# A gated cross-attention layer with a routed feed-forward part on one Trainium2 core: where the first batches' feed-forward part is done, the last row sums, and the opening loads

## The chip, the cores and the metric

The kernel runs on one core of a Trainium2 chip, as one program from its first load to its last store. The metric is device time in microseconds (us). A core has five engines with a queue of instructions each: TensorE (PE; its weight loads are listed apart as PEld), VectorE (DVE), ScalarE (ACT), GpSimd (POOL) and SyncE (SP). SP, ACT and POOL also issue DMA transfers. Each queue runs in its own order, and an instruction that waits holds up all that stand behind it. Products are accumulated in eight PSUM banks of 128 x 512 numbers.

## What is computed

Four batches of 256 tokens (x, 512 wide) attend to 1601 context rows each. 32 query heads share 8 key and value heads, four to one. Then each token goes through a base product and two of eight small experts. All of it is in float32.

```python
def _L0_xattn_ref(query, kv, Wq, bq, Wkv, bkv, Wo, bo):
    scale = 1 / sqrt(128)
    q = (query @ Wq + bq).reshape(B, L, 8, 4, 128)
    k_, v_ = jnp.split(kv @ Wkv + bkv, 2, axis=-1)
    k, v = k_.reshape(B, Lk, 8, 128), v_.reshape(B, Lk, 8, 128)
    scores = jnp.einsum('blkgd,bmkd->bkglm', q, k) * scale
    attn = jax.nn.softmax(scores, axis=-1)
    o = jnp.einsum('bkglm,bmkd->blkgd', attn, v).reshape(B, L, 4096)
    return o @ Wo + bo

def _L0_ffn_ref(x, base_W, router_W, lora_A, lora_B):
    base = jnp.einsum('bsd,od->bso', x, base_W)
    probs = jax.nn.softmax(jnp.einsum('bsd,ed->bse', x, router_W), axis=-1)
    top_vals, top_idx = jax.lax.top_k(probs, 2)
    rw = top_vals / jnp.sum(top_vals, axis=-1, keepdims=True)
    w_dense = jnp.sum(jax.nn.one_hot(top_idx, 8) * rw[..., None], axis=-2)
    mid = jnp.einsum('bsd,edr->bser', x, lora_A) * w_dense[..., None]
    return base + 2.0 * jnp.einsum('bser,erd->bsd', mid, lora_B)

x = x + jnp.tanh(g_xattn[0]) * _L0_xattn_ref(_layernorm(x), ctx_4096, Wq, bq, Wkv, bkv, Wo, bo)
x = x + jnp.tanh(g_ffn[0]) * _L0_ffn_ref(_layernorm(x), base_W, router_W, lora_A, lora_B)
```

## The kernel before

A *group* is one key head h of one batch b and one half l of its tokens: the four query heads of 128 tokens each make 512 columns (W). There are 4 x 8 x 2 = 64 groups, and the loop over `heads` and l runs them in order. A group's scores are 13 products (12 context tiles of 128 rows and one of 65), one PSUM bank each (`score_unit`, L880). ACT copies them to SBUF (L887) into tiles named p, two context tiles to one p, seven p to a group. DVE takes the maximum over the p (tile mx, `fold`, L806 to L812), spreads it to all partitions (`spread`, L845 to L839, result mb), and subtracts it (L915). ACT takes the exponential in place (L918), and TensorE multiplies with the values (`av_unit`, L967) while the next group's scores are made. DVE adds the same p up (tile sm, again `fold` and `spread`, with small copies on POOL) and scales the result by the inverse sums (`normalize`, L1017). ACT adds the value bias (oT, L1020), TensorE projects with the output weights (po, L1033), and DVE adds that to x in the tile xa (L1040). There are nine buffers for p, so that a copy of the next group's scores may have to wait until DVE has added up a p of the group before.

Between two groups lies a *window* of other work, held as tasks: projection, queries of the next head (pq, L531), keys and values of the next pair of heads (pxk, pxv and others), the next batch's context and x, and the feed-forward part. The order on TensorE, DVE and ACT is written out by hand (`manual_schedule`): a planner in the kernel keeps a clock per engine with costs of its own, gives each task a share of the windows before it is due, and takes the step that is ready first. `flush` does the same at the end without windows. DMA issues on SP and POOL are placed by the compiler's scheduler.

**Feed-forward part** (`ffn_steps`), for each of the eight tiles of 128 tokens: row statistics and normalisation on DVE (fn, L265 to L272), four transposes (pt_f, L248), a product with LoRA A and the router weights (pm, L1093), routing on DVE (`weigh`, L1114 to L1130) and one exponential on ACT (L1106), one transpose (pmt, L1140), the base product (py, L1085) and the LoRA B product into the same bank (L1152), the sum into xa (L1153) and the store. The first three batches' parts run in the windows of the batch that follows; the last batch's runs at the end. Its weights (base_t, ra, lb) stay in SBUF from the start: `ffn_weight_steps` loads them in the opening and transposes the base weights in the first groups.

**The last group** (7,1 of batch 3) has its p in the place of the context (p_last). It has no sums on DVE: after each value product, a product of the same p with a matrix of ones adds the sums up on TensorE (su, L980), 13 of them. `turn_over` turns these sums round (L1002 to L1005). The group before it (7,0) still uses DVE and POOL. The output weights wo have one buffer; `load_wo` of a head is called after the projection of the head before.

**The opening** loads 13 context tiles of batch 0 one at a time on SP (`load_first`, L1314), the first key weights and the bias on ACT's queue (L300, L220), and the first value weights, x, query and output weights on SP. TensorE transposes each tile (pt_ctx). The first key product (pk, L575) needs the short tile 12 and tiles 0 to 2.

Of the kernel before, what the change touches and what calls it, by code (L numbers as in the profile page):

```python
# [27 lines left out]
def flamingo_kernel(  # L28
# [190 lines left out]
    def load_small():  # L219
        nc.scalar.dma_start(bias[0:NHEAD], bq.rearrange("(h p) -> h p", p=P))  # L220
        nc.scalar.dma_start(bias[NHEAD:NBIAS], bkv.rearrange("(h p) -> h p", p=P))
        nc.gpsimd.dma_start(gates[:, 0:1], g_xattn.partition_broadcast(P))
        nc.gpsimd.dma_start(gates[:, 1:2], g_ffn.partition_broadcast(P))
        nc.gpsimd.dma_start(bo_b, bo.partition_broadcast(P))
# [95 lines left out]
    def load_wo(b, h):  # L320
        o = pool.tile([P, G, D], F32, tag="wo", name=f"wo_{b}_{h}", bufs=1)
# [6 lines left out]
    base_t = const.tile([P, NC, D], F32, name="base_t")  # L328
    ra = const.tile([P, NC, E * R + E], F32, name="ra")
    lb = const.tile([E * R, D], F32, name="lb")  # L330

    router_s = pool.tile([P, NL, D], F32, tag="xa", name="router_s")

    def ffn_weight_steps():
        staged = {}

        def load(o):
            n = P if o < NC else E

            if o == NC:  # L340
                s = router_s[:, 0, :]
            else:
                s = pool.tile([P, D], F32, tag="stage", name=f"base_{o}", bufs=STAGE)
# [3 lines left out]
        def begin():  # L347
            for c in range(NC):
                nc.gpsimd.dma_start(
                    ra[:, c, : E * R].rearrange("p (e r) -> p e r", r=R),  # L350
                    lora_a[:, c * P : (c + 1) * P, :].rearrange("e p r -> p e r"),
                )
            nc.sync.dma_start(lb, lora_b.rearrange("e r d -> (e r) d"))
            load(0)

        def step(o):
            def run():
                if o < NC:
                    load(o + 1)
                    dst, n = base_t[:, :, o * P : (o + 1) * P], P  # L360
                else:
                    dst, n = ra[:, :, E * R :], E
                transpose_rows(staged.pop(o), n, dst, f"base_{o}")
            return NC * TR_COST, LAG_DMA, run, True

        return [(0, 0, begin)] + [step(o) for o in range(NC + 1)]
# [7 lines left out]
    def x_steps(b):  # L374


        def begin():
            xa = pool.tile([P, NL, D], F32, tag="xa", name=f"xa_{b}")
# [516 lines left out]
    last = (B - 1, NKV - 1, NL - 1)  # L895
    assert (NPAIR - 1) * 2 * W <= NC * 2 * HW

    def softmax(key):
# [10 lines left out]
        for j, tiles in enumerate(pairs):  # L909
# [12 lines left out]
            if key != last:  # L922
                first = NPAIR - FULL // 2
                ns = 0 if j <= first else 1230 if j > first + 1 else 1970 if first else 1230
                later("sum", "v", ns, ("exp", key, j), lambda j=j: sum_piece(key, j), ("sum", key, j))
        if key != last:
            later("sum", "v", 0, 0.0, lambda: sum_spread(key), ("sums", key))

    def sum_piece(key, j):
        if j == 0:  # L930
            nm = "_".join(map(str, key))
            acc_t[key] = pool.tile([P, 2, W], F32, tag="sm", name=f"sm_{nm}", bufs=1)
# [18 lines left out]
    def av_unit(key, j):  # L951
# [22 lines left out]
        if key == last:  # L974

            if j == 0:
                sum_t[key] = bank(f"su_{nm}")
            for k, i in enumerate(pairs[j]):
                r = rows[i]
                nc.tensor.matmul(  # L980
                    sum_t[key],
                    ones[:r],
                    p_t[key][j][:r, k, :],
                    start=(j == 0 and k == 0),
                    stop=(j == NPAIR - 1 and k == len(pairs[j]) - 1),
                )
        if j == NPAIR - 1 and key != last:
            done["av", key] = clock["now"] + SEM
        elif key == last and j == NPAIR - 1:
            turn_over(key)  # L990

    def av_step(key, j):

        return 2 * len(pairs[j]) * mm_cost(W), ("exp", key, j), lambda: av_unit(key, j), j == 0

    def turn_over(key):

        nm = "_".join(map(str, key))
        rb = pool.tile([P, W], F32, tag="stage", name=f"rb_{nm}", bufs=STAGE)
        tr = pool.tile([P, W], F32, tag="stage", name=f"tr_{nm}", bufs=STAGE)  # L1000
        m = small.tile([P, NB], F32, tag="quadm", name=f"quadm_{nm}", bufs=2)
# [458 lines left out]
```

## Time and profile before

| what | value |
|---|---|
| median of three runs | 2665.49 us (2664.94 to 2667.97) |
| the profiled execution | 2665.57 us, of which its span 2663.8 us |
| mean granted TensorE clock | 0.997 |
| DVE's additions and maxima over p (sm, mx) | each about 1.22 us for 128 x 1024 numbers |
| ACT's copies of scores (L887) | 820, 0.59 us each, 463.4 us |
| TensorE's score products | 1664 passes, two to a product |
| mean DMA rate | 39 GB/s over the span |

The span runs from the first to the last instruction on the core. The other 1.8 us of the profiled execution lie around it. A float32 product is listed as two passes over TensorE, so that "x8" in a row is four products; rows overlap by the time a product takes to drain, so the time a step costs is read from one row's start to the next one's. The page shows the span in 40 slices, the busy share in tenths, and the granted clock; a full slice is 66.6 us:

```profile
PE   8999999999999999999999999999999999999997
DVE  2787877888878778778878878788887787888785
ACT  2544444454444344445444444444544444444441
PEclk9999999999999999999999999999999999999998
```

TensorE is nearly full everywhere but in the first and the last slice; DVE is at 70 to 80%.

### The profile page before, as it was taken

Reading aid. Unit: us, or ns where it says so; the run is one execution under the profiler, and the core shown is the slowest. Engines: PE = TensorE matmul, PEld = TensorE weight load, DVE = VectorE, ACT = ScalarE, POOL = GpSimd, SP = SyncE. Lnnn points to the kernel's source line nnn. Section 1 sums busy time; section 2 is a strip of 40 time slices with the busy share of each in tenths; the row PEclk is TensorE's granted clock in tenths of the full one; section 3 lists DMA queues with packets and bytes.
Section 4 is the critical chain, followed back from the end, with each engine's and each line's share of the span. In section 5 each row is a group of like instructions: output and inputs, shape, how many; then the busy total and the mean of one; then the engine's idle time right before and its main releaser. Section 6 shows DMA issues by size and latency. Waiting matters only on the chain.

```text
span 2663.8 us, 25411 instructions
## 1 busy us (share of the span) xinstructions
PE 2614.0 (98%) x9127; PEld 1480.4 (56%) x9127; DVE 2101.9 (79%) x3074; ACT 1200.5 (45%) x1920; POOL 92.3 (3%) x404
## 2 busy tenths in 40 slices
PE   8999999999999999999999999999999999999997
PEld 6555565655655556556555555556565564655543
DVE  2787877888878778778878878788887787888785
ACT  2544444454444344445444444444544444444441
POOL 0000000000000000000000000000000000000000
PEclk9999999999999999999999999999999999999998
DMA  3101111120111011112001010111210010100000
GB/s 127 53 17 40 40 32 40 40 74 24 40 32 40 25 39 40 40 32 89 24 24 40 32 56 8 40 40 44 70 40 21 28 48 32 40 25 24 32 16 24
DMA packets 78263, 104.72 MB, mean 39 GB/s; under 512 B 3324, under 2 KB 36140, under 8 KB 78136
## 3 DMA queue, kind: packets, MB, share of 16 engines
q1 hardware_dynamic: 76728, 102.01, 12.1%
q8 instruction: 72, 1.18, 0.2%
q0 software_dynamic: 272, 0.53, 0.1%
q10 hardware_dynamic: 1136, 0.55, 0.1%
q14 instruction: 55, 0.45, 0.1%
HBM read 100.98 MB, written 2.10 MB: 39 GB/s over the span
## 4 chain that ended last, share of the span: by engine, by line
PE 77%; DVE 15%; ACT 5%; issue 1%; POOL 1%; DMA 1%; SPq 0%; ACTq 0%; POOLq 0%; DVEq 0%
PE av L967 20%; PE sc L880 20%; PE po L1033 8%; PE pq L531 6%; PE pxk L665 5%; PE pxv L676 4%; DVE p L915 4%; PE pk L575 3%; ACT p L887 3%; PE pyk L665 2%; PE pyv L676 2%; DVE sm L812 2%; DVE mx L812 2%; ACT p L918 1%; PE pzk L665 1%
## 5 line engine op out<-in xcount | busy, mean ns | idle before, releaser
L880 PE MATMUL sc<-qT,kT 128*128 128x512 f32 (+1 forms) x1664 | 776.1, 592 | 7.7 <-ACT p L887 4.8
L887 ACT COPY p<-sc 65x512 f32<-65x512 f32 x820 | 463.4, 590 | 679.6 <-PE sc L880 348.4
L967 PE MATMUL av<-p,v 65*128 65x512 f32 x1640 | 766.1, 592 | 3.0 <-ACT p L918 3.0
L967 PEld LDWEIGHTS av<-p,v 65*128 65x128 f32 x1640 | 309.3, 190 | 382.6 <-issue 377.5
L880 PEld LDWEIGHTS sc<-qT,kT 128*128 128x128 f32 (+1 forms) x1664 | 306.3, 186 | 379.6 <-issue 334.4
L812 DVE TENSOR_TENSOR mx<-mx,p 128x1024 f32<-128x1024 f32 x252 | 308.8, 1226 | 237.8 <-ACT p L887 235.6
L918 ACT ACTIVATE p<-p 65x512 f32<-65x512 f32 x442 | 434.6, 995 | 124.6 <-DVE p L915 116.4
L915 DVE TENSOR_TENSOR p<-p,mb 65x512 f32<-65x512 f32 x442 | 481.8, 1137 | 0.2
L812 DVE TENSOR_TENSOR sm<-sm,p 128x1024 f32<-128x1024 f32 x252 | 307.2, 1219 | 1.3
L1033 PE MATMUL po<-wo,oT 128*128 128x512 f32 x512 | 231.7, 596 | 5.3 <-DMA wo<-in_L_xattn_Wo_dram 5.3
L531 PE MATMUL pq<-xnT,wq 128*128 128x256 f32 x1024 | 231.5, 379 | 0.0
L531 PEld LDWEIGHTS pq<-xnT,wq 128*128 128x128 f32 x1024 | 193.0, 190 | 38.6 <-issue 6.5
L1033 PEld LDWEIGHTS po<-wo,oT 128*128 128x128 f32 x512 | 95.5, 191 | 109.8 <-issue 105.8
L703 ACT ACTIVATE kT<-pxk,biasT 128x384 f32<-128x384 f32 (+1 forms) x120 | 60.7, 526 | 174.9 <-PE pxk L665 174.9
L706 ACT COPY v<-pxv 128x384 f32<-128x384 f32 x120 | 57.0, 475 | 166.7 <-PE pxv L676 166.7
L829 POOL COPY quad_sm<-quad_sm 32x16 f32<-32x16 f32 x189 | 46.6, 246 | 2363.9 <-DVE quad_sm L825 2217.4
L538 ACT ACTIVATE qT<-pq,biasT 128x256 f32<-128x256 f32 x128 | 60.6, 474 | 149.9 <-PE pq L531 149.3
L806 DVE TENSOR_TENSOR mx<-p,p 128x1024 f32<-128x1024 f32 x63 | 77.2, 1226 | 57.2 <-ACT p L887 57.2
L676 PE MATMUL pxv<-wv,T 128*128 128x128 f32 x720 | 91.4, 277 | 9.4 <-ACT v L706 9.4
L676 PEld LDWEIGHTS pxv<-wv,ctxT 128*128 128x128 f32 x720 | 88.7, 192 | 20.2 <-issue 18.4
L575 PE MATMUL pk<-ctxT,wk 128*128 128x417 f32 (+1 forms) x256 | 90.9, 509 | 2.8 <-ACT ctxT L250 1.5
L676 PEld LDWEIGHTS pxv<-wv,T 128*128 128x128 f32 x720 | 86.3, 192 | 12.4 <-ACT v L706 11.7
(158 smaller groups left out, 2284.4 us busy)
## 6 DMA issues: line engine op xcount, KB each, us to landing
wq<-in_L_xattn_Wq_dram SPq DMA_DIRECT2D x32, 1024.0 KB, 5.3
wo<-in_L_xattn_Wo_dram SPq DMA_DIRECT2D x32, 1024.0 KB, 5.3
ctx<-in_ctx_dram SPq DMA_DIRECT2D x48, 256.0 KB, 2.7
wk<-in_L_xattn_Wkv_dram SPq DMA_DIRECT2D x30, 256.0 KB, 2.9
wv<-in_L_xattn_Wkv_dram SPq DMA_DIRECT2D x30, 256.0 KB, 3.0
xa<-in_x_dram SPq DMA_DIRECT2D x4, 512.0 KB, 3.7
out_dram<-xa SPq DMA_DIRECT2D x8, 256.0 KB, 2.0
base<-in_L_ffn_base_W_dram SPq DMA_DIRECT2D x4, 256.0 KB, 6.1
```

The costliest lines, as they stand in the source:

```text
L531: nc.tensor.matmul(pq[:, :L], w_t["q", b, h][:, c, g * HDIM : (g + 1) * HDIM], xnT_t[b][:, c, :], start=(c == 0), stop=(c == NC - 1),)
L575: nc.tensor.matmul(pk[:, :n], w_t["k", b, h // 2][:, raw_slot(h % 2, c), c % 2, :], ctxT_t[b][:, c, lo : lo + n], start=(c == 0), stop=(c ...
L665: nc.tensor.matmul(bk[:, :n], a(SLOT[i], c), operand(i, c, s, n), start=first and c == 0, stop=c == 1, skip_group_check=True,)
L676: nc.tensor.matmul(bk[:, t * HDIM : (t + 1) * HDIM], operand(i, c, s + t * P, P), a(SLOT[i], c), start=first and t == 0 and c == 0, stop=c ...
L806: nc.vector.tensor_tensor(acc, p[first], p[first + 1], op)
L812: nc.vector.tensor_tensor(acc, acc, p[j], op)
L880: nc.tensor.matmul(sc[:r, :], kT_t[b, h][:, key_col(i) : key_col(i) + r], qT_t[b, h][:, :, l * P : (l + 1) * P], start=True, stop=True,)
L887: nc.scalar.copy(p[:r, k, :], sc[:r, :])
L915: nc.vector.tensor_tensor(p, p, m, ALU.subtract)
L918: nc.scalar.activation(p, p, AF.Exp, scale=scale)
L967: nc.tensor.matmul(av, v_t[b, h][:r, i, :], p_t[key][j][:r, k, :], start=(j == 0 and k == 0), stop=(j == NPAIR - 1 and k == len(pairs[j]) ...
L1033: nc.tensor.matmul(po, oT_t[key][:, g, :], w_t["o", b, h][:, g, :], start=(g == 0), stop=(g == G - 1),)
```

## The change

- **Feed-forward part.** The feed-forward part of batches 0 to 2 is no longer done in the windows of the next batch. Only its row statistics are (`early_stats`), into two small tiles. x keeps a tile for each batch (xa, four buffers), so all four x loads can be issued at once. From group (5,1) of the last batch on, when the tile of context sums (tag T) and a weight tile (tag wkv) are free, the feed-forward weights are loaded and transposed there (`ffn_weight_steps`, now waiting for the last pair of value heads). All six tiles are normalised (`early_norms`), transposed and multiplied with the router weights as tasks due within four windows. Their routing is done for all six at once on 6 x 8 numbers a row (`early_weights`). Their base and last products are `spare` tasks, which no window takes and `flush` does at the end, ranked behind other work that is ready as early.
- **Last sums.** For the last two groups DVE adds the p up as it does elsewhere, but the sum over partitions is a product with ones (`su_steps`): two products for (7,0) over the finished tile sm; for (7,1) two over the sum of all p but the last, and two over the last p.
- **Output weights of the last head** are loaded into the query weights' buffer, once the last queries are made.
- **Opening.** Context tiles are loaded two to a transfer. The order on SP is now tile 12, tiles 0 and 1, tiles 2 and 3, value weights, tiles 4 to 11, x, query weights. The bias is loaded on POOL's queue. Six products of the identity with itself stand first on TensorE. The LoRA weights leave the opening.

The core of the diff:

```diff
     def load_small():
-        nc.scalar.dma_start(bias[0:NHEAD], bq.rearrange("(h p) -> h p", p=P))
-        nc.scalar.dma_start(bias[NHEAD:NBIAS], bkv.rearrange("(h p) -> h p", p=P))
+        nc.gpsimd.dma_start(bias[0:NHEAD], bq.rearrange("(h p) -> h p", p=P))
+        nc.gpsimd.dma_start(bias[NHEAD:NBIAS], bkv.rearrange("(h p) -> h p", p=P))
...
     def load_wo(b, h):
-        o = pool.tile([P, G, D], F32, tag="wo", name=f"wo_{b}_{h}", bufs=1)
+        tag = "wq" if (b, h) == heads[-1] else "wo"
+        o = pool.tile([P, G, D], F32, tag=tag, name=f"wo_{b}_{h}", bufs=1)
...
-        return [(0, 0, begin)] + [step(o) for o in range(NC + 1)]
+        return [(0, ("pair", "v", B - 1, NKV // 2 - 1), begin)] + [step(o) for o in range(NC + 1)]
...
-            xa = pool.tile([P, NL, D], F32, tag="xa", name=f"xa_{b}")
+            xa = pool.tile([P, NL, D], F32, tag="xa", name=f"xa_{b}", bufs=B)
...
+    def su_steps(key):
+        nm = "_".join(map(str, key))
+        end = NPAIR - 2 if key == last else NPAIR - 1
+        def add(tiles, start, stop):
+            if start:
+                sum_t[key] = bank(f"su_{nm}")
+            for k, p in enumerate(tiles):
+                nc.tensor.matmul(
+                    sum_t[key], ones[: p.shape[0]], p,
+                    start=start and k == 0, stop=stop and k == len(tiles) - 1,
+                )
...
+        acc = lambda: [acc_t[key][:, k, :] for k in range(2)]
+        steps = [(2 * mm_cost(W), ("sum", key, end), lambda: add(acc(), True, key != last), True)]
         if key == last:
-            if j == 0:
-                sum_t[key] = bank(f"su_{nm}")
-            for k, i in enumerate(pairs[j]):
-                r = rows[i]
-                nc.tensor.matmul(
-                    sum_t[key],
-                    ones[:r],
-                    p_t[key][j][:r, k, :],
-                    start=(j == 0 and k == 0),
-                    stop=(j == NPAIR - 1 and k == len(pairs[j]) - 1),
-                )
...
+            tiles = lambda: [p_t[key][-1][: rows[i], k, :] for k, i in enumerate(pairs[-1])]
+            steps.append(
+                (len(pairs[-1]) * mm_cost(W), ("exp", key, NPAIR - 1), lambda: add(tiles(), False, True))
+            )
...
+            if h == NKV - 1 and b < B - 1:
+                later("low", "v", 1000, t, lambda: early_stats(b, l))
...
-            if l == NL - 1 and n < len(heads):
+            if l == NL - 1 and n + 1 < len(heads):
                 load_wo(*heads[n])
         return [(G * mm_cost(D), ("oT", key), project, True)] + (
-            ffn_steps(b, l) if h == NKV - 1 else []
+            ffn_steps(b, l) if (b, h) == heads[-1] else []
         )
...
+    def early_norms():
+        rs = small.tile([P, N_EARLY], F32, tag="rs6", name="rs6", bufs=1)
+        later("low_a", "a", 1500, 0.0, lambda: nc.scalar.activation(sd6, sd6, AF.Sqrt), "sd6")
+        later("ln", "v", 200, "sd6", lambda: nc.vector.reciprocal(rs, sd6), "rs6")
...
+            later("ln", "v", 700, "rs6", run, ("ln", f"f_{b}_{l}"))
...
+        if i < 2:
+            base[0] = (half * mm_cost(D), ("xT", nm), base[0][2], True)
+            return route, base + final
+        return route, final[:1] + base + final[1:]
...
-            t = min(left, key=lambda t: max(t.ready, clock["now"]))
+            t = min(left, key=lambda t: max(t.ready, clock["now"]) + t.spare * t.steps[0][0] / 2)
...
-            t.credit = t.cost() / (later_ + 1) if later_ > 0 else NEVER
+            t.credit = 0 if t.spare else t.cost() / (later_ + 1) if later_ > 0 else NEVER
...
-    load_first(0)
+    load_first(FULL)
     load_pair("k", 0, 0, eng=nc.scalar)
-    load_first(1)
+    warm = bank("warm")
+    for i in range(6):
+        nc.tensor.matmul(warm[:, :P], ident, ident, start=True, stop=True)
+    give(0.0)
+    load_first(0, 2)
+    load_first(2, 2)
     load_small()
-    load_first(2)
-    load_first(3)
...
+    for i in range(4, FULL, 2):
+        load_first(i, 2)
     xs = x_steps(0)
     xs.pop(0)[2]()
-    for n in range(4, KT):
-        load_first(n)
     load_wq(*heads[0])
...
-            if now == 0:
-                tasks.append(Task(ffn_weight_steps()))
+            if (b, h, l) == (B - 1, NKV - 3, NL - 1):
+                tasks.append(Task(ffn_weight_steps() + [(0, 0, early_norms)]))
+                both = [ffn_steps(*t) for t in early]
+                tasks[:0] = [Task(route, now + 4) for route, _ in both]
+                tasks.extend(Task(steps, spare=True) for _, steps in both)
...
-            if l == NL - 1 and hi + 2 < len(heads):
-                load_wq(*heads[hi + 2])
+            if l == NL - 1 and nxt is not None:
+                if hi + 2 < len(heads):
+                    load_wq(*heads[hi + 2])
+                else:
+                    load_wo(*nxt)
+    tasks.insert(0, Task(su_steps(prev)))
     run_group(last, prev, 4)
-    tasks.insert(0, Task(out_steps(prev)))
+    tasks.insert(1, Task(out_steps(prev)))
     tasks.insert(0, Task([av_step(last, j) for j in range(NPAIR)] + out_steps(last)))
+    tasks.insert(0, Task(su_steps(last)))
     flush(lambda t: True)
```

## The prediction

> **What bounds the kernel now.** I read the page's busy times first, then the stages, then TensorE's waits in the end and in the middle, then single rows.
>
> ```profile
> PE 2614.0 (98%) x9127; PEld 1480.4 (56%) x9127; DVE 2101.9 (79%) x3074; ACT 1200.5 (45%) x1920; POOL 92.3 (3%) x404
> ```
>
> TensorE (PE) is busy for all but 49.8 us of the span. So work taken from it in the middle should come back one for one, if nothing else is close behind. The next view cuts heads 1 to 7 of each batch out of the run, first batch first (columns: stretch, its length, busy PE, PEld, DVE, ACT, POOL, clock, DMA share, GB/s).
>
> ```profile
> 189.40:547.80 358.40, 356.14 (x1290) 205.31 (x1289) 287.56 (x395) 161.08 (x256) 12.61 (x54) 1.00 0.11 36
> 829.00:1198.30 369.30, 365.21 (x1312) 209.23 (x1311) 295.11 (x431) 162.30 (x258) 11.98 (x54) 1.00 0.12 38
> 1479.40:1848.50 369.10, 365.30 (x1313) 209.32 (x1312) 295.12 (x431) 162.38 (x258) 11.99 (x54) 1.00 0.12 38
> 2129.70:2498.90 369.20, 365.16 (x1312) 209.18 (x1311) 295.08 (x431) 162.28 (x258) 11.93 (x54) 1.00 0.11 36
> ```
>
> The first batch has no feed-forward part to do there; the other three each do that of the batch before. They are 10.9, 10.7 and 10.8 us longer. The first batch is thus a measured copy of what these heads cost without it. The end is different: there TensorE waits.
>
> ```profile
> PE po L1033 <- DMA wo<-in_L_xattn_Wo_dram: 5.3, 1, 5.3
> PE pmt L1140 <- DVE mid L1130: 4.5, 1, 4.5
> PE av L967 <- ACT p L918: 3.0, 2, 1.8
> PE sc L880 <- ACT qT L538: 2.3, 1, 2.3
> PE pm L1093 <- DVE fT L253: 1.7, 2, 1.0
> PE pt_f L248 <- DVE fn L272: 1.5, 1, 1.5
> PE py L1152 <- ACT midT L1142: 0.7, 2, 0.4
> ```
>
> These are all its waits from 2508 us on: 19.0 us. Its granted clock (third column from the end) falls after two of them:
>
> ```profile
> 2566.40:2597.80 31.40, 28.38 (x66) 11.91 (x65) 29.39 (x44) 17.17 (x25) 0.00 (x0) 1.00 0.00 1
> 2597.80:2601.20 3.40, 3.40 (x6) 1.38 (x5) 3.40 (x4) 3.17 (x4) 0.00 (x0) 0.51 0.00 0
> 2601.20:2628.60 27.40, 22.38 (x52) 9.56 (x51) 19.55 (x27) 5.22 (x6) 2.27 (x12) 1.00 0.12 38
> 2628.60:2632.00 3.40, 3.08 (x4) 1.50 (x5) 0.00 (x0) 0.00 (x0) 0.00 (x0) 0.50 0.00 0
> 2632.00:2663.80 31.80, 19.68 (x59) 8.86 (x57) 14.59 (x54) 2.90 (x9) 0.00 (x0) 0.88 0.05 17
> ```
>
> **What moves.** Per tile of 128 tokens the feed-forward part costs TensorE four transposes (0.43 us from one row to the next), the router product (0.95), the base product (885.88 to 889.32, 3.44), its last product (0.86) and one transpose (0.11): 5.79 us. Six tiles are 34.7 us, and five transpositions of base weights 2.1 us. The instruction orders of the two built programs agree on TensorE, but for these and six warming products, up to head 5 of the last batch.
>
> **1. The middle: -40.7 us.** Heads 1 to 7 lose 10.9 + 10.7 + 10.8 = 32.4 by the comparison above. Head 0 loses two groups of four transposes and two router products per batch, 2 x (0.43 + 0.95) x 3 = 8.3. This includes a wait of 1.6 us in each of three batches, in which the router's arithmetic on DVE delays the row sums and so the copies that free the score banks:
>
> ```profile
> 860.08 1.13 PE L880 MATMUL sc<-qT,kT 128*128 128x512 f32 x2 [1.60 <-ACT p L887]
> ```
>
> What would be late next is DVE, with 288 of 358 us busy; the first batch shows that it holds. The row statistics (0.69 + 0.18 + 0.15 us a tile) stay in the middle, on DVE, as before. Eight activation tables of 1.28 us fewer are loaded on ACT, which is 45% busy: nothing.
>
> **2. The first group: -2.1 us,** the base transposes between the scores of head 0. Their loads and those of the LoRA weights leave the opening's queues.
>
> **3. The opening: -1.5 us,** from +1.0 to -3.4.
>
> ```profile
> 11.09 1.12 PE L248 MATMUL pt_ctx<-ident,ctx 128*128 128x128 f32 x4 [2.01 <-DMA ctx<-in_ctx_dram]
> 13.20 5.12 PE L575 MATMUL pk<-ctxT,wk 128*128 128x417 f32 x8 [0.99 <-DVE ctxT L253]
> ```
>
> The first key product waits for context tile 2, issued at 2.1 us and landed at 11.05. Afterwards tiles 2 and 3 are one transfer issued at about 1.9. The only transfer of that shape, the load of x, took 10.1 us to land: 12.0, a loss of 1.0. The nearer tile, ctx 1, landed at 7.69, a gain of 3.4. I take a gain of 1.5, because the four LoRA loads (64 KB each, 9.2 us to landing) that shared the engines are gone. From 20 to 65 us TensorE is busy for 41.5 of 45.4 us, so the gain lasts. The x load, moved behind all context tiles on SP, is first used by DVE at 23.3 us; all tiles issued ahead of it are 4.5 MB, 13 us at the 350 GB/s of the better slices, so it lands before 20. The three later x tiles, now loaded at once, fall where DMA is idle (28 us on). The bias, now on GpSimd's queue, is needed after tile 1; its neighbours there landed 6.1 to 7.3 us after issue, on ACT's 5.5: hidden by the wait for tile 2, which is later. The six warming products end before the first tile can be used. [...]
>
> The same rows show a slow clock: eight passes took 5.12 us at 13.2, against 2.85 us for eight such passes at 27.3. I take no gain from the warming products: 12 passes of 0.22 us at that rate are 2.7 us, and then TensorE waits again. If they open it, up to 2.1 us more.
>
> **4. The end, from 2508.9 us: +21.9 us.**
> - Work in: 34.7 + 2.1 = +36.8.
> - Sums: products with ones fall from 13 to 6 (2 for the last but one group, 4 for the last); 7 x 0.86 = -6.0. DVE gets 5.6 us of additions for it (1.23 + 0.69 + 3 x 1.22), in a stretch where it is idle for 28.5 of 62.6 us (the three rows from 2601.2 on).
> - The 19.0 us of waits go: the output weights are loaded into the query weights' place long before (-5.3), and other tiles' products lie in the gaps (-13.7).
> - Slow clock: two stretches of 3.4 us at half, and the last two products (2.07 + 0.48 us for what takes 1.12 + 0.27 elsewhere): -4.6.
> - New waits. (B) After group (6,1), two tiles' transposes stand ahead of the projection on TensorE. They need rows normalised on DVE behind its last maximum:
>
> ```profile
> 2532.27 1.23 DVE L812 TENSOR_TENSOR mx<-mx,p 128x1024 f32<-128x1024 f32 x1 [1.22 <-ACT p L887]
> ```
>
>   It ends at 2533.5, TensorE's last value product at 2531.2. DVE adds about 1.8 us (base copies, reciprocal) and 0.55 for the row, TensorE 2.1 of transposes: wait 2.5. Behind it stand the projection and the queries of head 7, +0.8. (C) The same after (7,0): maximum to 2569.98, product to 2566.39, DVE 0.9 us earlier by its order, 0.55 for the row: wait 3.3. (D) Then 1.0 for the first exp, 0.6 for the transposed copies, 1.0 and 1.6 where the six tiles' weights and the sums' additions queue on DVE, 1.6 + 0.7 for the last tile's router. Together +13.0. DVE's new small operations (128x48) have no row; 128x8 takes 0.16 to 0.23, 128x128 0.29, so twenty cost 3.2 to 5.8; I take 4.4, inside the 1.0. B and C would be nothing if DVE kept up, and 4 each if both rows had to be ready; D lies between 1.6 and 13.
> - Clock: the wait nearest to C's 3.3 us that was followed by a slow stretch is 1.8 (5.3 too); that nearest to B, 2.3 us, was not. One stretch: +1.7. [...]
>
> 36.8 - 6.0 - 19.0 - 4.6 + 13.0 + 1.7 = +21.9. The LoRA loads (4 x 0.88 us on GpSimd) stand ahead of copies of a row sum there; they can start at 2508.9 and end at 2512.4, before DVE asks at 2512.9. Late, they cost up to 3.5. On SP base, router and output weights have 5.3 us and more before their use.
>
> **Sum.** 2663.8 - 40.7 - 2.1 - 1.5 + 21.9 = 2641.4 us span. The profiled execution took 2665.57, 1.8 more than its span and within 0.1 of the median: 2643.2.
>
> **Rivals.**
> - *Better still* (0.12): B and C vanish, and the opening's clock and loads come at their best: 2643.2 - 7.5 - 4.0 = 2632. For it: the last value products of a group run 3.4 us past its last score, time in which DVE could finish. Against: in the row above it is 2.3 us behind them already.
> - *The end takes half again as long* (0.08): D at its upper bound, a second slow stretch, late LoRA loads: +7 + 1.7 + 3.5 = 2655.
> - *DVE becomes the bound in the middle* (0.05): half of the 40.7 comes back: 2663.5, no change. Against: batch 0.
> - *The end runs in a line* (0.05, slower): each tile's steps go from TensorE to DVE and back, and nothing lies over them. DVE's added 27 us (six times 2.6, base copies 2.9, additions 5.6, small ones 4.4, less the spread) add to TensorE's 30.8, and the old waits stay: 2663.8 - 44.3 + 57.8 = 2677 span, 2679. It decides once the end grows by more than 44.3 us. Against: DVE's 28.5 idle us there.
> - That the change doesn't do what it says is excluded by the instruction order.
>
> **Numbers.** Main case 0.70, 2643, its own range 2634 to 2653. With the neighbours 80% lie in 2632 to 2654. Faster by over 0.2% (5.3 us, about what a measurement can tell from no change) 0.90, within 0.05, slower 0.05.
>
> **What would show it.** Heads 1 to 7 of batches 1 to 3 last 358 to 359 us; the waits of 1.6 us are gone; TensorE waits for the normalised rows (pt_f) 2 to 4 us twice; none for output weights; the first key product starts near 11.7; from its first score of group (6,1) to the end the span is about 177 us instead of 154.9. I am wrong if these heads stay above 365 us, or if the last stretch passes 199.

## The result and the profile after

The changed kernel takes 2635.55 us (median of 4 runs, 2634.76 to 2636.84), the kernel before 2665.22 (4 runs, 2662.45 to 2667.97): a ratio of 0.9889, with a 95% interval of 0.9872 to 0.9906. The forecast was 2643.2, in a range of 2632 to 2654. The profiled execution took 2636.84 us, its span 2635.1; that of the kernel before was 2663.8, so 28.7 us went where 22.4 were forecast.

The page's busy times of the changed kernel:

```profile
PE 2608.0 (99%) x9125; PEld 1480.3 (56%) x9125; DVE 2090.8 (79%) x2991; ACT 1187.5 (45%) x1896; POOL 96.4 (4%) x400
```

TensorE does the same work but for a few products (2608.0 us against 2614.0); the other 22.7 us of the 28.7 were idle time, 27.1 us now against 49.8. To see where, I cut both spans at two marks, the first score of all and the first score of group (6,1) of the last batch (plain arithmetic on start times in the timeline of TensorE):

```
                 first score   first score to (6,1)   (6,1) to the end    span
before                65.35          2443.52               154.93       2663.8
changed               63.64          2395.83               175.63       2635.1
difference            -1.71           -47.69               +20.70        -28.7
predicted             -1.5            -42.8                +21.9         -22.4
```

The opening and the end came as forecast to within 1.2 us; the middle gave 4.9 us more. Heads 1 to 7 of each batch in the changed kernel, cut at the same instructions as in the prediction (columns as there: stretch, length, busy PE, PEld, DVE, ACT, POOL, clock, DMA share, GB/s):

```profile
185.40:542.46 357.06, 356.13 (x1290) 205.30 (x1289) 287.20 (x395) 160.01 (x254) 12.62 (x54) 1.00 0.11 36
820.93:1178.51 357.58, 356.15 (x1290) 205.32 (x1289) 287.17 (x395) 160.06 (x254) 12.55 (x54) 1.00 0.11 36
1456.88:1814.03 357.15, 356.23 (x1291) 205.40 (x1290) 287.29 (x395) 160.01 (x254) 12.57 (x54) 1.00 0.11 36
2092.49:2449.50 357.01, 356.08 (x1290) 205.25 (x1289) 287.15 (x395) 160.01 (x254) 12.62 (x54) 1.00 0.11 36
```

All four batches are now alike. But they are not like the first batch before (358.40): that one got faster too, by 1.34 us, though nothing was taken out of its heads 1 to 7. Its timeline on TensorE holds a wait that the prediction did not list. First the kernel before, then the changed one (columns: start, length, engine, line, operation, tiles, shape, count, and in brackets the idle time ahead and what ended it):

```profile
199.05 1.60 PE L676 MATMUL pxv<-wv,T 128*128 128x128 f32 x12 [1.64 <-ACT v L706]
```

```profile
193.71 1.60 PE L685 MATMUL pxv<-wv,T 128*128 128x128 f32 x12 [0.31 <-ACT v L715]
```

The same wait stood at this place in every batch. All of TensorE's waits at pxv (what ended them, us in total, times), before and then after, went from 9.4 us to 4.2, a fall of 5.2:

```profile
  ACT v L706: 9.4, 12
```

```profile
  ACT v L715: 4.2, 12
```

TensorE's waits in the end of the changed kernel, from group (6,1) on (columns: engine, tile and line, what ended the wait, us in total, times, longest):

```profile
PE pt_f L248 <- DVE ffn_x L1155: 2.7, 1, 2.7
PE pt_f L248 <- DVE ffn_w L1155: 2.1, 1, 2.1
PE av L979 <- ACT p L928: 2.0, 2, 1.2
PE pmt L1269 <- DVE lm L1258: 1.3, 1, 1.3
PE su L1003 <- DVE sm L821: 1.2, 1, 1.2
PE sc L889 <- ACT qT L547: 0.7, 1, 0.7
PE py L1282 <- ACT midT L1274: 0.4, 1, 0.4
PE pm L1214 <- DVE ffn_x L253: 0.3, 1, 0.3
PE pmt L1269 <- DVE lm L1138: 0.2, 1, 0.2
PE py L1282 <- ACT ffn_w L1274: 0.2, 1, 0.2
```

No wait for the output weights is left, and the two new waits at pt_f stand where the prediction put B and C. One slow stretch (about 3.4 us at half the granted clock) follows C, from 2525.30 to 2528.72 us: the projection there takes 4.86 us for eight passes that take 3.60 elsewhere.

```profile
2524.82 1.57 PE L248 MATMUL pt_f<-ident,ffn_x 128*128 128x128 f32 x8 [2.74 <-DVE ffn_x L1155]
2526.18 4.86 PE L1052 MATMUL po<-wo,oT 128*128 128x512 f32 x8
```

### The profile page after: what moved, and what is told of

Its sections match the earlier page's. It is cut to its first block, busy times and chain, and to the rows that moved or that the text cites. A ratio compares the mean times of both kernels' runs of the same rounds, so it can differ in the third digit from the quotient of the medians.

```text
span 2635.1 us, 25287 instructions
## 1 busy us (share of the span) xinstructions
PE 2608.0 (99%) x9125; PEld 1480.3 (56%) x9125; DVE 2090.8 (79%) x2991; ACT 1187.5 (45%) x1896; POOL 96.4 (4%) x400
## 4 chain that ended last, share of the span: by engine, by line
PE 80%; DVE 12%; ACT 5%; issue 1%; POOL 1%; DMA 0%; ACTq 0%; POOLq 0%; DVEq 0%
PE av L979 21%; PE sc L889 21%; PE po L1052 8%; PE pq L540 7%; PE pxk L674 5%; PE pxv L685 4%; PE pk L584 3%; DVE p L925 3%; ACT p L896 3%; PE pyk L674 2%; PE pyv L685 2%; DVE sm L821 2%; DVE mx L821 2%; ACT p L928 1%; PE pzk L674 1%
## 6 DMA issues: line engine op xcount, KB each, us to landing
ctx<-in_ctx_dram SPq DMA_DIRECT2D x6, 512.0 KB, 11.7
```

## The experiments

### Where the extra 4.9 us of the middle came from

**e4_no_middle** is the kernel before with the feed-forward part of three batches left out.

```diff
-            ffn_steps(b, l) if h == NKV - 1 else []
+            ffn_steps(b, l) if (b, h) == (B - 1, NKV - 1) else []
```

> The kernel before without the feed-forward part of batches 0 to 2 (their rows of the output are not computed); the transposes of the base weights stay in the first group of scores, and the end is as it was. From the first score to the first score of the second group of head 6 of the last batch the kernel before takes 2443.52 us, the changed kernel 2395.83, which is 4.9 us more than the 42.8 that the prediction took off (40.7 + 2.1). Theory (the 4.9 us are four waits of TensorE for a copy of the values, 1.64 us each before and 0.31 after, once per batch, because VectorE's additions are queued later where extra work stood in head 0): here the waits shrink to 0.31 us in batches 1 to 3 and stay 1.64 us in batch 0, where the base transposes still stand; the stretch takes 2399.0 to 2399.9 us. Rival (the prediction's sum was right for what was removed, and the 4.9 us came with another part of the change): all four waits stay, and the stretch takes 2402.3 to 2403.3 us.

From the first score to group (6,1) it took 2399.10 us, in the theory's interval. TensorE's waits in head 1 of batch 0, and then the same stretch of batch 1:

```profile
PE pxv L676 <- ACT v L706: 1.6, 1, 1.6
...
PE pxv L676 <- ACT v L706: 0.3, 1, 0.3
```

Batch 0, which kept the base transposes, kept its 1.64 us wait; batches 1 to 3 lost theirs. What links it to work that stood a group or two earlier is VectorE's queue. Here it is some 30 us ahead of the wait, first in e4_no_middle, where the wait remains, then in the changed kernel, where it is gone:

```profile
168.06 1.22 DVE L812 TENSOR_TENSOR sm<-sm,p 128x1024 f32<-128x1024 f32 x1
169.19 1.22 DVE L915 TENSOR_TENSOR p<-p,mb 128x1024 f32<-128x1024 f32 x1
170.33 0.42 DVE L316 TENSOR_TENSOR wv<-wv 128x256 f32<-128x256 f32 x1
170.66 0.69 DVE L845 TENSOR_TENSOR sm<-sm 128x512 f32<-128x512 f32 x1
```

```profile
160.10 4.62 DVE L925 TENSOR_TENSOR p<-p,mb 128x1024 f32<-128x1024 f32 x4
164.64 0.68 DVE L854 TENSOR_TENSOR sm<-sm 128x512 f32<-128x512 f32 x1
165.36 0.71 DVE L855 STREAM_TRANSPOSE sm<-sm 128x512 f32<-128x512 f32 x1
```

One addition of the row sums (sm, 1.22 us) is left over in the first queue and stands ahead of the last subtraction; in the second it was done earlier, when VectorE had room. In batches 1 to 3 the feed-forward part's rows had pushed it back, as e4_no_middle shows by leaving them out; that the copies of base tiles did the same in batch 0 is read from the queue. Everything behind it on VectorE, and so the score copies, the exponentials and the copy of the values on ScalarE, comes about 1.3 us later against TensorE: the first maximum of group (1,1) starts 11.9 us after that group's first score in batch 0 of e4_no_middle, and 10.6 us in its batches 1 to 3 and in every batch of the changed kernel. Four such shifts, 1.33 + 3 x 1.29, make 5.2 us. Group by group, e4_no_middle and the changed kernel agree: in each of batches 1 to 3 both lose 1.37, 1.36, 1.29 (1.28) and 10.67 us in the same four groups.

### The end: weights and sums

**e5_wo** is the kernel before with the last head's output weights loaded early, and nothing else.

```diff
-        o = pool.tile([P, G, D], F32, tag="wo", name=f"wo_{b}_{h}", bufs=1)
+        tag = "wq" if (b, h) == heads[-1] else "wo"
+        o = pool.tile([P, G, D], F32, tag=tag, name=f"wo_{b}_{h}", bufs=1)
...
+                else:
+                    load_wo(*nxt)
```

> The kernel before, with one part of the change alone: the output weights of the last head are loaded into the place of the query weights, a head earlier. Theory (the wait of 5.34 us for them stood on the path with nothing behind it, and the slow stretch after it was its doing): from the first score of the second group of head 6 to the end 147.9 us (without the slow stretch) to 149.6 us (with one elsewhere), instead of 154.93; time lower by 5.3 to 7.0 us. Rival (the row sums and the normalised outputs on VectorE and ScalarE would have been late by nearly as much): 152 us or more, time lower by less than 3 us.

The end took 147.93 us, 7.0 less than before, and the time fell to 2658.64 us (6 runs) against 2666.03 (9 runs): a ratio of 0.997, interval 0.9958 to 0.9982. The three last projections now stand in a row, at full rate (24 passes, 0.43 us each):

```profile
2619.55 10.62 PE L1034 MATMUL po<-wo,oT 128*128 128x512 f32 x24
```

So the wait of 5.34 us was on the path, with the slow stretch behind it (granted clock 0.50 from 2628.6 to 2632.0 us in the kernel before): a quarter of what the change gained, by an edit of a few lines.

**e6_sums** is the changed kernel with all sums of the last group on TensorE.

```diff
-            if key == last and j == NPAIR - 1:
+            if key == last:
                 continue
...
+        return [part(j) for j in range(NPAIR)]
```

> The changed kernel with all the sums of the last group on TensorE, as before: 13 products with ones instead of 4, and no additions for that group on VectorE; the sums of the group before stay as changed. Theory (the end is set by TensorE's work, as the prediction counted it): 9 products of 0.86 us more, so that the end, from the first score of the second group of head 6, takes 181.5 to 184 us instead of the 173.9 to 176.2 of the changed kernel and its variants so far; time 6 to 8.5 us higher. Rival (VectorE sets the end, and 5.6 us of additions go from it): 173 to 178 us, time the same within 3 us.

The end took 182.14 us, 6.5 more than in the changed kernel's profile, and the time was 2643.14 us (4 runs, 2641.05 to 2643.34), 7.6 above the changed kernel's 2635.55. Nine products of 0.86 are 7.7, and the wait of 1.2 us at su is gone, which leaves 6.5; from the first score of the last group to the end it is 6.3 us more (106.8 against 100.5). TensorE's work sets the end, as the prediction counted it, though VectorE had fewer additions here.

### The end: the two waits for normalised rows

**e7_po_first** puts the kept rows' transposes behind the projection.

```diff
         turned, second = [("ln", f"f_{nm}")], [("mid", nm) if i is None else "mid6"]
+        if i is not None:
+            turned.append(("po", B - 1, *((NKV - 3, 1) if i < 2 else (NKV - 2, 0))))
```

> The changed kernel with the transposes of the kept rows queued behind the output projection in the two places where TensorE waits for the normalised rows (2.10 us after the second score group of head 6, 2.74 us after the first of head 7). Theory (these waits stand on the path and have no other cause than the order): both fall under 0.3 us, the slow stretch behind the second goes too, and the time falls by 4.0 to 6.5 us, to 2629 to 2632 us. Rival (VectorE's work sets the end, so that a wait taken away here comes back further on): the time falls by less than 1.5 us and the waits in the last 60 us grow by 3 us or more.

Neither theory nor rival as it was put: 2634.10 us (4 runs, 2632.70 to 2636.12), 1.45 below the changed kernel, with an end of 173.14 us. Both waits at pt_f are gone, but a wait of 2.14 us is new, with a slow stretch behind it (granted clock 0.77 from 2531.0 to 2534.6 us and 0.84 from there to 2540.0), and the wait for the queries grew from 0.72 to 1.79 us:

```profile
PE sc L889 <- DVE xa L1059: 2.1, 1, 2.1
PE sc L889 <- ACT qT L547: 1.8, 1, 1.8
```

The scores wait for a bank that the projection holds until VectorE has added it to the residual, and that addition stands in VectorE's queue behind the chain from the last maximum to its spread. TensorE's order was not the cause: VectorE is late there, and TensorE meets it at the next place. The theory was wrong in this; the rival was right in its mechanism, not in its place, since the last 60 us kept their waits.

**e8_act** is e7_po_first with the filling products of e3_fill (below), and with the kept rows' copies moved from VectorE to ScalarE.

```diff
-            done["xT", nm] = transpose_rows(xn, P, xT, f"f_{nm}")
+            done["xT", nm] = transpose_rows(xn, P, xT, f"f_{nm}", i is not None)
```

> The changed kernel with the seven filling products of e3_fill, the order of e7_po_first, and the copies of the kept rows' transposes made by ScalarE instead of VectorE (six copies of 0.6 us). Theory (in e7_po_first VectorE's queue was the bound, and so the waits came back as 1.79 us for the queries' copy and 2.14 us for the residual's addition): these two fall to 0.8 us and under 1 us, the end takes 169.5 to 172 us, and the time is 2629 to 2632 us. Rival (the end has slack against VectorE only later on): the end takes 173 us or more, and the time is 2633 us or more.

2630.05 us (4 runs, 2629.24 to 2631.72): a ratio of 0.9866 to the kernel before, interval 0.985 to 0.9882. None of its runs overlaps with the changed kernel's, so it beats both. Of the 6.9 us between its profiled span and the changed kernel's, 2.9 lie ahead of the first score (60.69 us) and 3.9 in the end. The end took 171.71 us, 1.4 less than in e7_po_first; ends of one and the same order scatter by more than that (last section), so what the moved copies alone are worth is not shown. The wait for the queries fell to 0.6 us as the theory said; the other one did not fall, it grew:

```profile
PE sc L889 <- DVE xa L1059: 3.7, 1, 3.7
```

VectorE's queue shows why (same columns as the timelines above):

```profile
2519.35 1.23 DVE L821 TENSOR_TENSOR mx<-mx,p 128x1024 f32<-128x1024 f32 x1 [1.22 <-ACT p L896]
...
2524.98 0.71 DVE L848 STREAM_TRANSPOSE mb<-quadm_mx 128x512 f32<-128x512 f32 x1
2525.61 0.71 DVE L1059 SCALAR_TENSOR_TENSOR xa<-po,gates,xa 128x512 f32<-128x512 f32 x1
```

The projection ended on TensorE at 2519.0, but its addition is queued behind the whole chain and runs at 2525.6.

**e11_early_add** is e8_act and lets the projection, and whatever else is as short, stand between the scores of head 7.

```diff
-            run_group(cur, prev)
+            run_group(cur, prev, most=G * mm_cost(D) if (b, h) == heads[-1] else NC * TR_COST)
```

> e8_act, and steps as long as a projection may stand between the scores of head 7, so that the projection, the kept rows' transposes and products and two base products come earlier, and the residual's addition stands ahead of the last maximum on VectorE. Theory (the 3.74 us wait for that addition is one of order, and removing it shortens the end): the wait falls under 0.5 us, the end takes 168 to 170 us instead of 171.7, the time is 2626.5 to 2629 us. Rival (the products moved forward are missing as cover behind, and the waits come back there): the waits behind the last scores grow by 3 us or more, and the time is 2630 us or more.

2630.59 us (4 runs, 2629.26 to 2631.93), no different from e8_act, with an end of 172.77 us. The wait for the addition is gone and another has come in its place, the rival's case; of TensorE's waits in the end the first is

```profile
PE av L979 <- ACT p L928: 4.5, 2, 3.2
```

These are the value products of group (7,0), which wait for its exponentials (1.2 us in e8_act): products that had covered those were spent earlier.

### The opening

**e1_cold** takes the six warming products out, **e2_single** loads the context tiles one at a time, **e3_fill** puts seven more warming products into TensorE's gaps.

```diff
-    for i in range(6):
-        nc.tensor.matmul(warm[:, :P], ident, ident, start=True, stop=True)
```

```diff
-            eng.dma_start(
-                two, ctx_kv[0, i * P : (i + n) * P, :].rearrange("(t p) d -> p t d", p=P)
-            )
+            for k in range(n):
+                eng.dma_start(two[:, k, :], ctx_kv[0, (i + k) * P : (i + k + 1) * P, :])
```

```diff
+        keep_warm({0: 3, 2: 1, 3: 3}.get(n, 0))
```

> The changed kernel without its six warming products; nothing else differs. In the changed kernel the first key product starts at 10.68 us, eight of them stand 0.69 us apart until about 16.4 us (later ones 0.35), and the first score starts at 63.64. Theory (the warming gives nothing): first score within 0.3 us of 63.64, key products as slow as there. Rival (the six products brought the full clock forward): the slow rows last 1 to 2 us longer and the first score starts at 64.7 to 65.7.

> The changed kernel with its context tiles of the first batch loaded one at a time, in the same order; nothing else differs. Theory (the opening gained because the four LoRA loads no longer share the DMA engines): first key product between 10.2 and 11.2 us, first score within 0.5 us of 63.64. Rival (two tiles in one transfer make the gain): the first key product goes back towards 13.2 us and the first score towards 65.35, the numbers of the kernel before.

> The changed kernel with seven more warming products, put into TensorE's three waits before the first key product (3, 1 and 3 of them), so that it is busy from 1.5 us on. Theory (what keeps the clock low until 16.4 us are the gaps): the eight first key products stand nearer to 0.35 than to 0.69 us apart, the first score starts at 61 to 62 us instead of 63.64, and the time falls by 1.6 to 2.8 us. Rival (the clock opens at its own time, or the loads set the pace): first score at 63.5 to 64.4, time the same within 0.8 us.

The first key product stands at 10.67 us in e1_cold, 10.90 in e2_single and 10.68 in the changed kernel: neither the warming nor the paired loads brought it forward from 13.20. The first scores are at 62.13, 62.74 and 63.64 us, and the difference lies in how long the eight passes of the first key product take, 4.43, 4.80 and 5.90 us. In e1_cold neither expectation was met: without the warming products the first score came 1.5 us earlier. Each of e1_cold, e2_single, e9_lora and e10_bias (below) was run once (2633.69, 2634.78, 2634.60 and 2638.73 us), so only their traces are used. The eight passes in the changed kernel, and then in e3_fill:

```profile
10.68 5.90 PE L584 MATMUL pk<-ctxT,wk 128*128 128x417 f32 x8 [0.99 <-DVE ctxT L253]
```

```profile
10.39 3.04 PE L584 MATMUL pk<-ctxT,wk 128*128 128x417 f32 x8 [0.32 <-DVE ctxT L253]
```

With the gaps filled they run at full rate, here and in e8_act and e11_early_add (3.04 us in all three); in the eleven other executions they took 4.43 to 5.90. This is the clock: the trace's record of it begins with its first change (the views' means count the time ahead of that as 1.00), and full clock begins at 16.51 us in the changed kernel, 13.48 in e1_cold, 14.46 in e2_single, but at 6.79, 4.88 and 5.19 in the three with the gaps filled. Six warming products with gaps behind them did not keep the clock open: in e9_lora full clock began at 4.78 us, half clock again at 8.20, and full clock at 15.02. In e3_fill the first score is at 60.89 us. The time is 2634.39 us (4 runs, 2632.74 to 2635.64), only 1.2 below the changed kernel and within the scatter of both, so the theory's 1.6 to 2.8 us are shown in the trace of the opening but not in the time.

**e9_lora** brings the four LoRA loads back into the opening, **e10_bias** puts the bias back on ScalarE's queue, **e12_bias_only** is the kernel before with the bias moved to GpSimd's queue.

```diff
+    for c in range(NC):
+        nc.gpsimd.dma_start(
+            lm6[:, c, : E * R].rearrange("p (e r) -> p e r", r=R),
+            lora_a[:, c * P : (c + 1) * P, :].rearrange("e p r -> p e r"),
+        )
```

```diff
-        nc.gpsimd.dma_start(bias[0:NHEAD], bq.rearrange("(h p) -> h p", p=P))
-        nc.gpsimd.dma_start(bias[NHEAD:NBIAS], bkv.rearrange("(h p) -> h p", p=P))
+        nc.scalar.dma_start(bias[0:NHEAD], bq.rearrange("(h p) -> h p", p=P))
+        nc.scalar.dma_start(bias[NHEAD:NBIAS], bkv.rearrange("(h p) -> h p", p=P))
```

> The changed kernel with the four LoRA loads put back into the opening, behind the other loads of GpSimd's queue, into a buffer that is used much later; nothing else differs. Theory (the prediction's: their absence brought the first key product forward): it goes from 10.68 us back to 12.5 us or later. Rival (the order of the loads on the queues brought it): it stays at 10.4 to 11.2 us.

> The changed kernel with the two loads of the bias back on ScalarE's queue; nothing else differs. Theory (the prediction's: this move is hidden, because the context tile is later): first key product at 10.4 to 11.2 us as in the changed kernel. Rival (the small pieces of these loads on ScalarE's queue are what held the context tiles back before): 12 us or later.

> The kernel before, with one part of the change alone: the two loads of the bias stand on GpSimd's queue instead of ScalarE's. Three executions of the old opening had their first key product at 13.05 to 13.60 us; openings with the bias on GpSimd had it at 10.27 to 11.07, but once at 13.32. Theory (the bias on ScalarE's queue holds the context tiles back): first key product at 10.3 to 11.3 us, first score 1.5 to 3 us earlier than 65.35, time 1 to 3 us lower. Rival (the tile's landing varies by itself, or the order of the later loads decides): 12.5 us or later, time the same within 1 us.

The first key product moved by 0.4 us with the LoRA loads back (11.07; e6_sums, whose opening is the changed kernel's, has 10.94), so their absence was not the reason for the gain. With the bias back on ScalarE's queue it stood at 12.43 us, 1.75 later, and with the bias alone moved away it stood at 10.27. Over all executions, the bias on ScalarE's queue goes with 12.43 to 13.60 us (four), on GpSimd's with 10.27 to 11.07 (nine) and once with 13.32: the bias has much to do with it, in two ways. TensorE transposes the bias (pb) ahead of the last context tile that it needs, and in e10_bias it waits for the bias itself. The changed kernel, and then e10_bias:

```profile
8.33 0.31 PE L228 MATMUL pb<-ident,bias 48*128 48x48 f32 x1 [0.38 <-DMA bias<-in_L_xattn_bkv_dram]
```

```profile
9.83 0.31 PE L228 MATMUL pb<-ident,bias 48*128 48x48 f32 x1 [1.66 <-DMA bias<-in_L_xattn_bkv_dram]
10.33 1.11 PE L248 MATMUL pt_ctx<-ident,ctx 128*128 128x128 f32 x4 [0.19 <-DMA ctx<-in_ctx_dram]
```

In the kernel before, the bias had landed at 7.96 us and TensorE waited 2.01 us for tile 2, which landed at 11.05; in e12_bias_only that tile landed at 7.97. That the bias had held the tile back rests on this one execution of e12_bias_only, and e7_po_first, with the bias on GpSimd's queue, waited 1.97 us for the same tile. Yet e12_bias_only took 2666.18 us (11 runs) against 2665.63 (15 runs), a ratio of 1.0001, interval 0.9992 to 1.001. Its profiled execution is the slowest of the eleven (2669.26 us); there the gain of the first key product went like this:

```profile
10.27 4.92 PE L575 MATMUL pk<-ctxT,wk 128*128 128x417 f32 x8 [0.98 <-DVE ctxT L253]
17.25 0.94 PE L248 MATMUL pt_ctx<-ident,ctx 128*128 128x128 f32 x4 [2.05 <-DMA ctx<-in_ctx_dram]
17.98 5.07 PE L620 MATMUL pv<-wv_first,ctxT 128*128 128x256 f32 x16
```

The next context tile was now late by 2.05 us, the value products behind it took 5.07 us instead of 3.62, and the first score came at 66.19. In the changed kernel, and in e2_single, which loads that tile by itself, it is issued ahead of the value weights and x, and no such wait follows. So what the bias gains needs the new order of loads as well; whether the other ten executions lost it in the same way is not known. What a single execution says here is limited: the one at 13.32 us is e7_po_first, whose opening has the changed kernel's instructions; its first score came at 65.38.

## Why the prediction was right, and where it was not

- **The middle, -40.7.** Right for what it counted. Head 0 lost 3 x (1.37 + 1.36) = 8.2 us (8.3 forecast). Heads 1 to 7 of batches 1 to 3 lost 11.7, 12.0 and 12.2 us by the windows, 35.9 in all, of which 3.9 are the shrunken waits; that leaves 32.0 (32.4 forecast). The waits of 1.6 us that the router caused are gone. The step that failed is "The first batch is thus a measured copy of what these heads cost without it", and with it "the first batch shows that it holds" of VectorE. The copy had a wait of its own of 1.64 us, which came from the base transposes' copies on VectorE in head 0. The comparison cancelled it, in all four batches: 5.2 us that were forecast at nothing. The wait was there to be read, as a total of 9.4 us at pxv over 12 waits, four of them much longer than the rest.
- **The first group, -2.1:** 2.3 measured.
- **The opening, -1.5:** 1.7 in the profile, by luck. The first key product came 2.5 us earlier (forecast 1.5), and its eight passes took 5.90 us instead of 5.12, which gave 0.8 back. "The four LoRA loads that shared the engines are gone" is worth at most 0.4 us at the first key product, so this reason was wrong. The bias was forecast as "hidden by the wait for tile 2, which is later"; in the changed kernel TensorE's last wait for a load ahead of the first key product is the 0.38 us for the bias, and none is for tile 2. The two bias loads took 4.7 to 7.4 us to land on ScalarE's queue (four executions) and 4.8 to 6.3 on GpSimd's (ten). That the warming products alone would give nothing was right, but they do not end before the first tile can be used: its transposes follow them without a gap at 4.18 us, and stand at 3.55 in e1_cold. The next tile is waited for in both, so it cost nothing. The "eight such passes" of 2.85 us are of 384 columns; those of 417 take 3.07. The size is inside the scatter: three executions of the old opening had their first score at 65.14 to 65.90 us, three of the new one at 63.62 to 65.38.
- **The end, +21.9:** 20.7. Sums and weights were worth what was forecast (e6_sums, e5_wo). New waits were 11.2 us instead of 13.0 (the terms listed there add up to 13.1): B 2.10 (2.5), the queries behind it 0.72 (0.8), C 2.74 (3.3), all of D 5.6 (6.5). One slow stretch was forecast at 1.7, and one came, behind C: from the first score of (7,0) to that of (7,1) the profiled execution took 36.1 us, e1_cold 34.4 without one. That there was one is chance, since B and C drew none to two in executions of the same order (last section). No wait of the list names the LoRA loads or the kept weights.
- **The rivals.** *Better still* is where the time landed (2635.55, between 2632 and the forecast), but not by its mechanism: B and C stayed. *VectorE becomes the bound in the middle* did not come: its 287 of 357 us hold. *The end runs in a line* did not come either; the end grew by 20.7, far from 44.3.

Of the total, 28.7 - 22.4 = 6.3 us: 5.2 from the waits for the values, 1.2 from the end, 0.4 from the opening and the first group, less 0.5 in the middle's own sum.

## What to carry to other kernels

A stretch without the work is a good price list for removing it, but read its own waits first: the change may remove their cause too. Work taken from an in-order queue that runs close behind the bound engine can give back more than its own time, as here, where additions that it had pushed back no longer stood in front of something urgent (5.2 us of waits for the values). Where a wait is for an engine that is late anyway, reordering the waiting engine can just move the wait, as in e7_po_first (2.14 us at the scores in place of 2.10 and 2.74 at the transposes) and e11_early_add (from 1.2 to 4.5 us at the value products): cover spent early was missing later. That taking work off the late engine pays more is not shown, since e8_act changed three things.

## What the runs showed of the hardware that was not expected

- **The same wait halves the clock in some executions and not in others.** The wait B of 2.10 us is in seven executions whose end runs in the same order up to there. In two of them (the changed kernel, e1_cold) the next group's scores start 39.0 us after those of (6,1), in five 40.7: one slow stretch more. Transposes and projection behind this wait, in the changed kernel and then in e2_single:

```profile
2486.35 1.08 PE L248 MATMUL pt_f<-ident,ffn_w 128*128 128x128 f32 x8 [2.10 <-DVE ffn_w L1155]
2487.27 3.60 PE L1052 MATMUL po<-wo,oT 128*128 128x512 f32 x8
```

```profile
2485.43 1.69 PE L248 MATMUL pt_f<-ident,ffn_w 128*128 128x128 f32 x8 [2.09 <-DVE ffn_w L1155]
2486.91 4.70 PE L1052 MATMUL po<-wo,oT 128*128 128x512 f32 x8
```

The trace's record of the clock tells the two apart. Within one execution all its changes lie whole multiples of 3.413 us from one another; from one execution to another they stand differently against the span's start (first full clock at 16.51 us in the changed kernel, at 14.46 in e2_single). Of the fourteen waits B and C in these seven executions, nine leave TensorE idle for 2.09 us or more inside one stretch between two such edges, and half clock follows each of them; the other five are divided by an edge, at most 2.01 us lie in one stretch, and none is followed by half clock. So e1_cold has no slow stretch there, e3_fill, e6_sums and e10_bias have two. The stretches at B in the changed kernel (TensorE busy for 1.40 us, idle for 2.01) and in e2_single (busy for 1.32, idle for 2.09), with the one behind each (columns as in the heads' view above):

```profile
2484.34:2487.75 3.41, 1.40 (x10) 1.15 (x11) 2.88 (x5) 0.15 (x1) 0.00 (x0) 1.00 0.00 0
2487.75:2491.16 3.41, 3.41 (x11) 1.68 (x10) 3.25 (x8) 0.00 (x0) 0.00 (x0) 1.00 0.00 0
```

```profile
2482.30:2485.71 3.41, 1.32 (x6) 0.50 (x5) 2.19 (x4) 1.07 (x2) 0.00 (x0) 1.00 0.00 0
2485.71:2489.12 3.41, 3.41 (x11) 2.20 (x9) 2.65 (x5) 0.00 (x0) 0.00 (x0) 0.50 0.00 0
```

These 2 us are no general bound: in the kernel before, the wait of 1.81 us had 1.41 us inside one stretch, with products of only 65 rows beside it, and half clock followed.

- **The middle hardly scatters.** From the first score to (6,1) eight executions of the changed kernel and its variants took 2395.74 to 2395.91 us, two more 2395.53 and 2395.62; the end of one and the same order took 173.87 to 176.54 (six executions), the opening up to its first score 63.62 to 65.38 (three). What a single profile can tell thus depends on the stage: here differences of some 0.4 us in the middle, but only of 2 to 3 us at both ends.
